# Seven block products in place of eight on the way up through a gated feed-forward layer (Macaron block, one Trainium2 core)

## The chip, the core and the metric

The kernel runs on one core of one Trainium2 chip. The core has a matrix engine (TensorE; PE in the profile, with its weight loads as PEld), a vector engine (VectorE, DVE), a scalar engine (ScalarE, ACT), a general engine (GpSimd, POOL), and a queue that issues most transfers (SyncE, SP). All work on a shared on-chip memory of 128 partitions; PE writes its sums to eight accumulation banks, which DVE and ACT read. The metric is the time in microseconds (us) of one execution; the median of three runs is compared.

## What is computed

`x` is [2, 512, 512]: 1024 rows of 512 features, float32. Six residual parts follow one another. The first and the third are the gated feed-forward layer that the change is in, with the same weights; between them lies a state-space layer, after them come a small memory layer, an attention layer and the memory layer again.

```python
def _L0_ffn_ref(x, w1, s1, w2, s2, w3, s3):
    ...
    W1 = dequant_q40(w1, s1, hidden, dim)      # hidden = 1376, dim = 512
    W3 = dequant_q40(w3, s3, hidden, dim)
    W2 = dequant_q40(w2, s2, dim, hidden)
    a = jnp.einsum('bsd,hd->bsh', x, W1)
    b = jnp.einsum('bsd,hd->bsh', x, W3)
    h = jax.nn.silu(a) * b
    return jnp.einsum('bsh,dh->bsd', h, W2)
...
x = x + 0.5 * _L0_ffn_ref(_layernorm(x, axis=-1), ...)
x = x + _L0_attn_ref(_layernorm(x, axis=-1), ...)
x = x + 0.5 * _L0_ffn_ref(_layernorm(x, axis=-1), ...)
```

The weights come packed: one int32 holds two signed 4-bit values, and one float scale belongs to 64 values. `dequant_q40` takes both nibbles out, multiplies by the scales and lays the values out in order.

## The kernel before

**Rows and tiles.** The 1024 rows are eight tiles `x[t]` of 128 rows by 512 features, four to each of the two batches. A layer first normalises the tiles (`norm_parts`, L130 to L185): on each tile the statistics (L142, L143, DVE), the root (L146, ACT), the reciprocal (L163, DVE), the centring (L153, DVE), then four transposes on PE (L175) and a copy by ACT (L179) into `hT[b]`, which holds a batch with the features on the partitions, as four blocks of 128 features by 512 rows.

**Going up.** The 1376 middle units are padded to 11 tiles of 128. For each tile `ht`, `ffn` takes the two up weights `w1` and `w3` (each four blocks of 128 features by 128 units), and for each batch forms `pa` (`fa` in the trace) and `pb` (`fb`), four f32 products of 128x128 by 128x512 each (L298). ACT takes the tanh of half of `pa` (L303), DVE makes (tanh + 1) * pa (L305) and multiplies by `pb` (L308): the gated value `act`, twice what silu(a) * b is. A tile thus has 16 products in each pass.

**Going down.** For each of the eight row tiles, 11 products add up in a bank (`fo`, L317), and DVE adds a quarter of it to `x[t]` (L321). In the first pass the next layer's normalisation of the tile follows right behind.

**The weights.** In the first pass (`n == 0`) they are unpacked: SP loads the packed values and the scales (`unpack_in`: four transfers of 128 KB for one up weight; `unpack_out`: one of 256 KB and four of 64 KB for a down weight), DVE takes out the nibbles (two operations of 64x512 for an up weight, L222 and L213; sixteen of 32x128 for a down weight), and multiplies by the scales (L241, L261). The unpacked tile is also written to HBM by ACT's queue (`keep`, L281), and the second pass (`n == 1`) loads it from there (`wk`, L120 and L125). The buffers for packed values and for scales have three slots each, up weights share 20 slots with the weights of the state-space layer, down weights 12.

**What sets the order.** Each engine works in order. Most of the program is put in order by a list scheduler that looks for what is ready, and may pull an operation ahead of earlier ones of another stage. Inside `in_order()` the order of PE, DVE, ACT and POOL is that of the program text. Before the change this holds for the down products, but not for the norm, the unpacking and the up products of the feed-forward layers, which the scheduler orders: in the first pass it runs the unpacking of the down weights between the gating operations of the later tiles. SP's order is the scheduler's in both versions. The accumulation banks are named by tags: `mm`, `dd`, `y` and `tr` have two each during the feed-forward layers.

Of the kernel before, what the change touches and what calls it, by code (L numbers as in the profile page):

```python
# [10 lines left out]
F32 = mybir.dt.float32  # L11
# [3 lines left out]
AF = mybir.ActivationFunctionType  # L15
ALU = mybir.AluOpType
AX = mybir.AxisListType

P = 128
NB, S, D = 2, 512, 512  # L20
NT = NB * S // P
NC = S // P
KD = D // P
# [2 lines left out]

HID = 1376
NHT = 11


NH, HP, NG = 128, 64, 8
# [12 lines left out]
class Step:  # L44


    def __init__(self, g, b, q):
        self.g, self.b, self.q = g, b, q
        self.ct = g * PAIRS + q
        self.h0 = 2 * self.ct  # L50
        self.n = f"{self.ct}_{b}"
# [7 lines left out]
class Kernel:  # L59
    def __init__(self, tc, ctx, a, out):  # L60
        self.tc, self.nc, self.a, self.out = tc, tc.nc, a, out
        nc = self.nc
        self.const = ctx.enter_context(tc.tile_pool(name="const", bufs=1))
        self.xpool = ctx.enter_context(tc.tile_pool(name="xpool", bufs=1))
        self.dram = ctx.enter_context(
            tc.tile_pool(name="scratch", bufs=1, space=bass.MemoryType.DRAM)
        )
        masks = self.const.tile([P, 4, P], F32, name="masks")
        nc.sync.dma_start(out=masks, in_=a["masks"])
        self.ident = masks[:, 0, :]  # L70
        self.upper = masks[:, 1, :]
        self.below = masks[:, 2, :]
        self.ones = masks[:, 3, :]
        self.eps = self.const.tile([P, 2], F32, name="eps")
        nc.vector.memset(self.eps[:, 0:1], EPS)
        nc.vector.memset(self.eps[:, 1:2], 4.0 * EPS)
        self.npool = ctx.enter_context(tc.tile_pool(name="npool", bufs=1))
        self.x = []
        for t in range(NT):
            xt = self.xpool.tile([P, D], F32, name=f"x{t}", tag=f"x{t}")  # L80
            nc.sync.dma_start(out=xt, in_=a["x"][t * P : (t + 1) * P, :])
            self.x.append(xt)

    @contextmanager
    def ssm_const(self):
# [158 lines left out]
    def unpack_out(self, pool, ht):  # L244

        nc = self.nc
        wi = pool.tile([P, D], I32, tag="wi", name=f"wi2_{ht}", bufs=3)
        sc = pool.tile([P, D], F32, tag="sc", name=f"sc2_{ht}", bufs=3)
        nc.sync.dma_start(out=wi, in_=self.a["q2"][ht])
        for qd in range(4):  # L250
            rows = slice(qd * 32, qd * 32 + 32)
            nc.sync.dma_start(
                out=sc[rows], in_=self.a["s2"][ht, qd].partition_broadcast(32)
            )
            cols = wi[rows].rearrange("p (a e) -> p e a", e=4)
            for e in range(4):

                low = ((43 * e + qd) // 2) % 2 == 1
                self.nibble(cols[:, e, :], cols[:, e, :], low)
        wt = self.w2pool.tile([P, D], F32, tag="w2", name=f"w2_{ht}")  # L260
        nc.vector.tensor_tensor(out=wt, in0=wi, in1=sc, op=ALU.mult)  # L261
        return wt

    def ffn(self, n, then=None):

        tc, nc = self.tc, self.nc
        first = n == 0
        if first:
            self.kept = {}

        def weight(which, ht):
            if first:
                t = (
                    self.unpack_out(pool, ht)
                    if which == 2
                    else self.unpack_in(pool, which, ht)
                )
                keep = self.dram.tile(
                    list(t.shape), F32, name=f"keep{which}_{ht}", tag=f"k{which}_{ht}"
                )  # L280
                nc.scalar.dma_start(out=keep, in_=t)  # L281
                self.kept[which, ht] = keep
                return t
            load = self.w2 if which == 2 else self.w
            return load(self.kept[which, ht], f"wk{which}_{ht}")

        with tc.tile_pool(name=f"ffn{n}", bufs=2) as pool:
            hT = self.norm(f"f{n}")
            act = []
            for ht in range(NHT):  # L290
                w1, w3 = weight(1, ht), weight(3, ht)
                g = pool.tile([P, NB, S], F32, tag=f"act{ht}", name=f"act{n}_{ht}", bufs=1)
                for b in range(NB):
                    pa = self.ps("mm", [P, S], f"fa{n}_{ht}_{b}")
                    pb = self.ps("dd", [P, S], f"fb{n}_{ht}_{b}")
                    for dst, wt in ((pa, w1), (pb, w3)):
                        for k in range(KD):
                            nc.tensor.matmul(  # L298
                                dst, lhsT=wt[:, k, :], rhs=hT[b][:, k, :],
                                start=k == 0, stop=k == KD - 1,  # L300
                            )
                    th = pool.tile([P, S], F32, tag="th", name=f"th{n}_{ht}_{b}", bufs=3)
                    nc.scalar.activation(th, pa, AF.Tanh, scale=0.5)  # L303

                    nc.vector.scalar_tensor_tensor(  # L305
                        out=th, in0=th, scalar=1.0, in1=pa, op0=ALU.add, op1=ALU.mult
                    )
                    nc.vector.tensor_tensor(out=g[:, b, :], in0=th, in1=pb, op=ALU.mult)  # L308
                act.append(g)
            w2 = [weight(2, ht) for ht in range(NHT)]  # L310
            with self.in_order():
                parts = then() if then is not None else None
                for t in range(NT):
                    b, c = divmod(t, NC)
                    po = self.ps("mm", [P, D], f"fo{n}_{t}")
                    for ht in range(NHT):
                        nc.tensor.matmul(  # L317
                            po, lhsT=act[ht][:, b, c * P : (c + 1) * P], rhs=w2[ht],
                            start=ht == 0, stop=ht == NHT - 1,
                        )  # L320
                    nc.vector.scalar_tensor_tensor(  # L321
                        out=self.x[t], in0=po, scalar=0.25, in1=self.x[t],
                        op0=ALU.mult, op1=ALU.add,
                    )
                    if parts is not None:
                        hT, start, turn = parts
                        start(t)
                        if t > 0:
                            turn(t - 1)
            return parts  # L330

    def in_order(self):
# [1059 lines left out]
def masks():  # L1392
    i = np.arange(P)
    m = np.zeros((P, 4, P), np.float32)
    m[:, 0] = i[:, None] == i[None]
    m[:, 1] = i[:, None] <= i[None]
    m[:, 2] = i[:, None] > i[None]
    m[:, 3] = 1
    return m
# [42 lines left out]
    return w.reshape(o // P, P, i // P, P).transpose(0, 3, 2, 1)  # L1442


def pad_hidden(v, axis):
    to = [(0, 0)] * v.ndim
    to[axis] = (0, NHT * P - HID)
    return np.pad(v, to)


def layout(v):
    a = {"x": v["L0_attn_x"].reshape(NB * S, D), "masks": masks()}
    later = np.arange(P)[:, None] < np.arange(P)[None]
    a["later"] = np.tile(later, (1, NC)).astype(np.float32)
    for n in (1, 3):
        w = pad_hidden(v[f"L0_ffn_w{n}"].reshape(HID, KD, 64), 0)
        s = pad_hidden(v[f"L0_ffn_s{n}"].reshape(HID, KD, 2), 0)
        a[f"q{n}"] = w.reshape(NHT, P, KD, 64).transpose(0, 3, 2, 1)
        a[f"s{n}"] = s.reshape(NHT, P, KD, 2).transpose(0, 3, 2, 1)
    w = v["L0_ffn_w2"]  # L1460
    w = pad_hidden(np.concatenate([w, w], axis=1).reshape(D, HID).T, 0)
    a["q2"] = w.reshape(NHT, P, D)

    s = np.repeat(v["L0_ffn_s2"], 2).reshape(D, HID // 32).T
    s = np.pad(s, ((0, NHT * 4 - HID // 32), (0, 0)))
    a["s2"] = s.reshape(NHT, 4, D)

    a["w_in"] = w_tiles(v["L0_attn_in_proj_w"])
# [9 lines left out]
        axis=1,  # L1478
# [23 lines left out]
    i = np.arange(P)  # L1502
# [24 lines left out]
```

## Time and profile before

| | us |
|---|---|
| median of three runs (lowest, highest) | 2854.03 (2848.28, 2856.74) |
| the profiled execution's own time | 2862.34 |
| its span, first to last instruction | 2860.6 |
| pass 1 of the feed-forward layer: first up product, first down product, end | 17.62, 169.06, about 247 |
| state-space layer | about 247 to 2160 |
| pass 2: first up product, first down product, end | 2169.84, 2323.87, about 2399 |
| memory, attention, memory | about 2399 to 2860 |
| mean granted clock of PE, share of full speed | 0.974 |

The span is what the profiler saw of one execution, and its own time lies 1.7 us above it. Busy shares count instructions from start to end; PE's records are pipelined, so that a record of 592 ns can be followed by the next after 429 ns, and one f32 product is two records. "Idle before" is the time in which an engine did nothing ahead of a group, with what released it. The granted clock is 1.00 at full speed.

### The profile page before, as it was taken

The page shows a single profiled execution, that of the slowest core. Times are in us where ns is not written, and L with a number is a line of the kernel's source. Part 1 is how long each engine was busy: PE and PEld are TensorE (multiplying, and loading weights), DVE is VectorE, ACT ScalarE, POOL GpSimd, SP SyncE. Part 2 cuts the span into 40 slices and gives each one's busy share as a digit, 9 for nine tenths or more (in the row PEclk, how much of TensorE's full clock was granted, in tenths as well). Part 3 has the DMA queues.
Part 4 walks back from the last instruction along what each step waited for, and adds up shares of the span by engine and source line. Part 5 has one row for each costly group of instructions (what it writes and reads, how often), then busy time and mean ns, then how long its engine had stood idle before and what let it go on. Part 6 is the DMA issues. An engine that isn't in the chain of part 4 may idle for free. (4 is left out here: it accounts for less than half of the span.)

```text
span 2860.6 us, 33568 instructions
## 1 busy us (share of the span) xinstructions
PE 2740.4 (96%) x12288; PEld 1420.1 (50%) x12288; DVE 1988.6 (70%) x3635; ACT 1070.8 (37%) x2355; POOL 529.8 (19%) x348
## 2 busy tenths in 40 slices
PE   8998899999999999999999999999998999788987
PEld 4444455555555555555555555555554444444443
DVE  6824777877888788787788788878882224555545
ACT  1012444444444344344444444434542002244332
POOL 0001112323323222131332322312220000100000
PEclk9999999999999999999999999999999999889986
DMA  8602223223223322322322422332230010000000
GB/s 243 208 33 81 87 87 129 96 76 133 94 82 118 114 81 102 127 85 90 128 92 75 139 96 82 111 122 81 90 110 15 0 49 33 0 1 1 1 1 30
DMA packets 75620, 237.78 MB, mean 83 GB/s; under 512 B 9824, under 2 KB 10400, under 8 KB 58944
## 3 DMA queue, kind: packets, MB, share of 16 engines
q1 hardware_dynamic: 70416, 226.00, 22.9%
q10 hardware_dynamic: 4752, 8.65, 0.8%
q8 instruction: 98, 1.61, 0.2%
q0 software_dynamic: 288, 0.98, 0.1%
q14 instruction: 66, 0.54, 0.1%
HBM read 223.80 MB, written 11.80 MB: 82 GB/s over the span
## 5 line engine op out<-in xcount | busy, mean ns | idle before, releaser
L509 PE MATMUL pg<-hT_s,wi 128*128 128x512 f32 x1024 | 472.3, 604 | 14.6 <-issue 6.9
L509 PE MATMUL cp_h<-hT_s,wi 128*128 128x512 f32 x1024 | 462.9, 595 | 0.0
L698 PE MATMUL po<-wo,yg 128*128 128x512 f32 x1024 | 460.7, 593 | 1.6 <-DVE yg L768 1.6
L600 DVE TENSOR_TENSOR_SCAN M<-rows,later 128x512 f32<-128x512 f32 x256 | 457.4, 1825 | 0.0
L775 POOL TENSOR_TENSOR ssum<-ssum,sq 128x512 f32<-128x512 f32 x112 | 142.5, 1272 | 1237.3 <-ACT sq L774 1237.3
L509 PEld LDWEIGHTS pg<-hT_s,wi 128*128 128x128 f32 x1024 | 184.3, 189 | 222.4 <-issue 214.6
L523 DVE SCALAR_TENSOR_TENSOR acc_h<-cp_h,small,acc_h 128x511 f32<-128x511 f32 (+2 forms) x384 | 286.2, 745 | 9.1
L509 PEld LDWEIGHTS cp_h<-hT_s,wi 128*128 128x128 f32 x1024 | 185.5, 191 | 185.1 <-issue 185.1
L698 PEld LDWEIGHTS po<-wo,yg 128*128 128x128 f32 x1024 | 184.8, 190 | 185.5 <-issue 183.6
L616 POOL TENSOR_TENSOR Cs<-CT,rows 128x768 f32<-128x768 f32 x128 | 254.6, 1989 | 46.3 <-DMA rows<-rows 31.5
L685 DVE SCALAR_TENSOR_TENSOR st<-st,dec_whole,st 128x64 f32<-128x64 f32 x512 | 108.8, 274 | 131.2 <-ACT st L680 131.2
L528 ACT ACTIVATE th_h<-acc_h 128x512 f32<-128x512 f32 x128 | 80.6, 630 | 296.4 <-DVE acc_h L523 296.4
L645 ACT ACTIVATE hd<-ht,dec_end 128x64 f32<-128x64 f32 x768 | 171.1, 324 | 38.3 <-DVE hc L637 38.3
L774 ACT ACTIVATE sq<-yg 128x512 f32<-128x512 f32 x112 | 70.7, 631 | 288.6 <-DVE yg L768 288.6
L614 DVE TENSOR_TENSOR M<-M,CB 128x512 f32<-128x512 f32 x256 | 164.5, 684 | 0.1
L605 ACT ACTIVATE M<-M 128x512 f32<-128x512 f32 x128 | 80.8, 631 | 193.2 <-DVE M L600 193.2
L637 DVE TENSOR_TENSOR hc<-ht,dt 128x512 f32<-128x512 f32 x128 | 88.1, 689 | 90.2 <-PE ht L792 90.2
L1265 DVE CUSTOM_DVE_ANT_0 j<-s,future 128x384 f32<-128x384 f32 (+3 forms) x256 | 112.8, 487 | 53.3 <-PE s L1255 53.1
L749 PEld LDWEIGHTS py<-M,hc 128*64 128x64 f32 x2048 | 109.2, 136 | 66.9 <-issue 64.7
L675 PEld LDWEIGHTS st<-hd,Btok 128*128 128x128 f32 x768 | 103.7, 191 | 75.0 <-issue 39.9
L749 PE MATMUL py<-M,hc 128*64 128x128 f32 x2048 | 140.1, 279 | 0.0
L740 POOL TENSOR_TENSOR x<-x,add 128x512 f32<-128x512 f32 x64 | 97.0, 1545 | 142.6 <-ACT add L738 142.6
(283 smaller groups left out, 3753.0 us busy)
## 6 DMA issues: line engine op xcount, KB each, us to landing
rows<-rows SPq DMA_DIRECT2D x128, 1024.0 KB, 4.7
wi<-in_w_in_dram SPq DMA_DIRECT2D x144, 256.0 KB, 2.8
wo<-in_w_out_dram SPq DMA_DIRECT2D x64, 256.0 KB, 3.4
keep<-w ACTq DMA_DIRECT2D x33, 256.0 KB, 3.5
wk<-keep SPq DMA_DIRECT2D x33, 256.0 KB, 2.7
wi<-in_q_dram SPq DMA_DIRECT2D x44, 128.0 KB, 3.9
sc<-in_s_dram SPq DMA_DIRECT2D x44, 128.0 KB, 3.9
wi<-in_q_dram SPq DMA_DIRECT2D x11, 256.0 KB, 2.8
```

The costliest lines, as they stand in the source:

```text
L509: self.nc.tensor.matmul(p, lhsT=wt[:, k, :], rhs=self.hT[b][:, k, :], start=k == 0, stop=k == KD - 1)
L523: self.nc.vector.scalar_tensor_tensor(out=acc[:, s:], in0=p[:, : S - s], scalar=w[:, 3 - s : 4 - s], in1=acc[:, s:], op0=ALU.mult, op1=ALU ...
L600: self.nc.vector.tensor_tensor_scan(out=m, data0=rows[:, i, 0, :], data1=self.later, initial=0.0, op0=ALU.add, op1=ALU.mult,)
L614: self.nc.vector.tensor_tensor(out=m, in0=m, in1=sh["CB"], op=ALU.mult)
L616: self.nc.gpsimd.tensor_tensor(out=cur.Cs, in0=sh["CT"][:, P:].unsqueeze(1).to_broadcast([P, 2, S - P]), in1=cur.rows[:, :, 1, P:], op=ALU ...
L645: nc.scalar.mul(hd[:, c, ch], p1.pt[:, c, ch], self.dec["dt_end"][:, b * NC + c, h0 + i : h0 + i + 1],)
L675: nc.tensor.matmul(pst[:, c, :], lhsT=self.sh[p1.g, p1.b]["Btok"][:, c, :], rhs=hd[:, c, :], start=True, stop=True,)
L685: nc.vector.scalar_tensor_tensor(out=st[:, c, ch], in0=st[:, c - 1, ch], scalar=self.dec["whole"][:, p1.b * NC + c, h : h + 1], in1=pst[:, ...
L698: nc.tensor.matmul(self.po[c], lhsT=p2.yg[:, c * P : (c + 1) * P], rhs=self.wo[p2.ct], start=p2.q == 0, stop=p2.q == PAIRS - 1,)
L749: nc.tensor.matmul(py[ch, cs], lhsT=hc[:, c, ch], rhs=p1.M[i].rearrange("p (c t) -> p c t", c=NC)[:, c, :], start=c == 0, stop=c == 0, ski ...
L775: nc.gpsimd.tensor_tensor(out=self.ssum, in0=self.ssum, in1=sq, op=ALU.add)
L1265: nc.vector.tensor_tensor_reduce(out=junk[:, :nk], in0=ps[y][:, at[i]], in1=self.future[:, S - nk :], scale=1.0, scalar=-3e38, op0=ALU.add ...
```

## The change

**The block product.** For one tile of middle units, take the up weights as a 2x2 block matrix: the two weights by the two halves of the features (blocks 0 and 1, blocks 2 and 3). Take the rows as another: the two halves of the features by the two batches. The four results (a and b, batch 0 and batch 1) are then a 2x2 by 2x2 block product, eight half products of two PE products each. The change writes it with seven (Strassen's method in Winograd's form, which shares sums): 14 PE products. Tile 0 stays as it was. Sums of the rows are formed once in a layer (`T`, four of 128x1024), sums of the weights once per tile and pass (`s` and `u`, two tiles with four sums of 128x256). Some sums of products are formed by letting PE go on adding in one bank `x`, out of which ACT copies the value in between (three times a tile: into `g`, `u2` and `u4`); the others are DVE additions.

**The order.** After the change, the whole layer is in `in_order()`. Batch 0 is normalised, the first up weights are unpacked, tile 0's products of batch 0 run, then batch 1 is normalised and tile 0's products of batch 1 run. After that, each tile has three parts: `begin` (four products from batch 0 alone), `middle` (six), `end` (four), and the `begin` of a tile stands ahead of the `end` of the tile before. The weights of the next tile are taken between, one down weight per tile at its end, and the writes of unpacked weights (`keep`) at fixed places. `x[4]` to `x[7]` are loaded behind the first up weights.

**The middle units** are reordered in blocks of 32 on the host (`hidden_tiles`), the same in w1, w3 and w2, so that all rows of a down weight's tile have the same nibble pattern. Then a tile's nibbles come out in two operations of 128x256 in place of sixteen of 32x128 (in two tiles of the eleven, in four operations). The unpacking of the up weights is unchanged.

```diff
-        self.x = []
-        for t in range(NT):
-            xt = self.xpool.tile([P, D], F32, name=f"x{t}", tag=f"x{t}")
-            nc.sync.dma_start(out=xt, in_=a["x"][t * P : (t + 1) * P, :])
-            self.x.append(xt)
+        self.x = [
+            self.xpool.tile([P, D], F32, name=f"x{t}", tag=f"x{t}") for t in range(NT)
+        ]
+        self.load(0)
+
+    def load(self, b):
+        for t in range(b * NC, (b + 1) * NC):
+            self.nc.sync.dma_start(out=self.x[t], in_=self.a["x"][t * P : (t + 1) * P, :])
...
-            cols = wi[rows].rearrange("p (a e) -> p e a", e=4)
-            for e in range(4):
-
-                low = ((43 * e + qd) // 2) % 2 == 1
-                self.nibble(cols[:, e, :], cols[:, e, :], low)
+        for kind, r0, r1 in HIDDEN[ht][1]:
+            cols = wi[r0:r1].rearrange("p (a e) -> p a e", e=4)
+
+            for low in (False, True):
+                e = [e for e in range(4) if ((43 * e + kind) // 2 % 2 == 1) == low]
+                part = cols[:, :, e[0] : e[1] + 1 : e[1] - e[0]]
+                self.nibble(part, part, low)
...
+        def product(dst, w, x, start=True, stop=True):
+
+            for k in range(2):
+                nc.tensor.matmul(
+                    dst, lhsT=w[:, k, :], rhs=x[:, k, :],
+                    start=start and k == 0, stop=stop and k == 1, skip_group_check=True,
+                )
+
+        def sums(ht):
+
+
+            w1, w3 = weight(1, ht), weight(3, ht)
+            lo, hi = slice(0, 2), slice(2, 4)
+            if ht:
+                s, u = (
+                    self.wpool.tile([P, KD, P], F32, tag="w", name=f"ws{i}{n}_{ht}")
+                    for i in range(2)
+                )
+                tt(s[:, lo], w3[:, lo], w3[:, hi], ALU.add)
+                tt(s[:, hi], s[:, lo], w1[:, lo], ALU.subtract)
+                tt(u[:, hi], w1[:, lo], w3[:, lo], ALU.subtract)
+                tt(u[:, lo], w1[:, hi], s[:, hi], ALU.subtract)
+                ws[ht] = w1, w3, s, u
+            else:
+                ws[ht] = w1, w3
...
+        def gated(g, a):
+
+            th = pool.tile([P, S], F32, tag="th", name="th", bufs=3)
+            nc.scalar.activation(th, a, AF.Tanh, scale=0.5)
+            nc.vector.scalar_tensor_tensor(
+                out=g, in0=th, scalar=1.0, in1=a, op0=ALU.add, op1=ALU.mult
+            )
+
+        def begin(ht):
...
+            product(x, w1[:, :2], hT[0][:, :2], stop=False)
+            nc.scalar.copy(g[:, 0, :], x)
+            product(r2, w1[:, 2:], hT[0][:, 2:])
+            tt(g[:, 0, :], r2, g[:, 0, :], ALU.add)
+
+        def middle(ht):
...
+            product(x, s[:, 2:], T[1], start=False, stop=False)
+            nc.scalar.copy(u2, x)
+            product(r7, u[:, 2:], T[2], stop=False)
+            product(x, s[:, :2], T[0], start=False, stop=False)
+            nc.scalar.copy(u4, x)
+            gated(act[ht][:, 0, :], act[ht][:, 0, :])
+            tt(u4, r7, u4, ALU.add)
+            st[ht] = x, r7, u2, u4
+
+        def end(ht):
...
+            product(x, u[:, :2], hT[1][:, 2:], start=False)
+            product(r7, w3[:, 2:], T[3], start=False)
+            gated(g[:, 1, :], x)
+            tt(g[:, 1, :], g[:, 1, :], u4, ALU.mult)
+            tt(u2, r7, u2, ALU.add)
+            tt(g[:, 0, :], g[:, 0, :], u2, ALU.mult)
+
+        with tc.tile_pool(name=f"ffn{n}", bufs=2) as pool, self.in_order():
...
+            def norms(b, then=()):
+                ts = range(b * NC, (b + 1) * NC)
+                for t in ts:
+                    stats(t)
+                    root(t, t + 1)
+                    if t > ts[0]:
+                        over(t - 1, t)
+                        centre(t - 1)
+                        turn(t - 1)
+                over(ts[-1], ts[-1] + 1)
+                centre(ts[-1])
+                turn(ts[-1])
+
+            norms(0)
+            sums(0)
+            if first:
+                self.load(1)
+            p0 = plain(0, 0)
+            norms(1)
+            p1 = plain(0, 1)
+            for b, (pa, pb) in enumerate((p0, p1)):
+                g = act[0][:, b, :]
+                gated(g, pa)
+                tt(g, g, pb, ALU.mult)
+
+            tt(T[0], hT[1][:, :2], hT[0][:, :2], ALU.subtract)
+            tt(T[1], hT[1][:, 2:], T[0], ALU.subtract)
+            sums(1)
+            tt(T[2], hT[1][:, 2:], hT[1][:, :2], ALU.subtract)
+            tt(T[3], hT[0][:, 2:], T[1], ALU.subtract)
+            keep()
+            w2.append(weight(2, 0))
+            for ht in range(1, NHT):
+                begin(ht)
+                if ht > 1:
+                    end(ht - 1)
+                keep()
+                if ht + 1 < NHT:
+                    sums(ht + 1)
+                middle(ht)
+                w2.append(weight(2, ht))
+            keep()
+            end(NHT - 1)
```

In `stats` and the rest, the steps of the norm are those of the kernel before. `plain` is the old product of tile 0 for one batch. The host's layout of w1, w3, w2 and their scales follows the new order of the middle units.

## The prediction, made before the change was run

> **What bounds the kernel now.** The page's first part says which engine is full, and the table of stages says it stage by stage.
>
> ```profile
> PE 2740.4 (96%) x12288; PEld 1420.1 (50%) x12288; DVE 1988.6 (70%) x3635; ACT 1070.8 (37%) x2355; POOL 529.8 (19%) x348
> ```
>
> Busy times of stages (start:end, length, then PE, PEld, DVE, ACT and POOL with instruction counts, granted clock, DMA share, GB/s); the rows are the up products of the first and of the second feed-forward pass:
>
> ```profile
> 17.60:168.60 151.00, 150.99 (x353) 66.71 (x352) 102.23 (x293) 16.50 (x26) 0.00 (x0) 1.00 0.64 201
> 2173.20:2323.40 150.20, 150.20 (x351) 66.51 (x350) 29.54 (x43) 16.31 (x26) 0.00 (x0) 1.00 0.01 4
> ```
>
> PE never pauses in either, at a granted clock of 1.00. A busy row alone could hide slack, so the timeline of PE gives the rate:
>
> ```profile
> 2179.67 3.60 PE L298 MATMUL fa<-hT_f,wk 128*128 128x512 f32 x8
> 2183.10 3.60 PE L298 MATMUL fb<-hT_f,wk 128*128 128x512 f32 x8
> ```
>
> Eight records start 3.43 us apart: 0.429 us a record, and an f32 product of 128x128 by 128x512 is two records (176 of `fa` for 88 products), 0.858 us. Fewer products mean less time, if PE stays fed. In pass 1 the feeder is DVE, which also unpacks:
>
> ```profile
> L213 DVE TENSOR_SCALAR wi<-wi 32x128 int32<-32x128 int32 x88 | 21.1, 270 | 0.4
> L222 DVE TENSOR_SCALAR wi<-wi 32x128 int32<-32x128 int32 x88 | 20.9, 269 | 0.1
> L241 DVE TENSOR_TENSOR w<-wi,sc 128x512 f32<-128x512 int32 x22 | 15.2, 691 | 2.4 <-DMA sc<-in_s_dram 1.6
> L305 DVE SCALAR_TENSOR_TENSOR th<-th,fa 128x512 f32<-128x512 f32 x22 | 15.1, 686 | 22.1 <-ACT th L303 21.9
> L213 DVE TENSOR_SCALAR wi<-wi 64x512 int32<-64x512 int32 x22 | 9.3, 424 | 8.9 <-DMA wi<-in_q_dram 8.3
> L261 DVE TENSOR_TENSOR w<-wi,sc 128x512 f32<-128x512 int32 x11 | 7.6, 689 | 0.2
> ```
>
> **The products.** A tile of 128 middle units has 16 products before (32 records, 13.73 us), and 14 after (28 records, 12.01 us). Tile 0 stays plain; ten tiles in two passes save 20 x 1.72 = **34.3 us**. All of it is on the path, since PE is the path. What gives some back:
>
> **DVE, per tile of pass 1.** Seven operations of 128x512 at 0.69 (the combining and gating) 4.8 us; two up weights, 2 x (0.42 + 0.41 + 0.69) = 3.0; four weight sums of 128x256; w2: two nibble operations in place of sixteen, and one product 0.69. The trace has no sum of two SBUF operands at 128x256; the nearest row is a 128x256 product:
>
> ```profile
> L1338 DVE TENSOR_TENSOR O<-po,r x16: 424/425/425, 2531.3 to 2779.7; 128x256 f32<-128x256 f32 x16
> ```
>
> So four sums are 1.7 us (1.1 by the 128-wide nibble row's 0.27, 2.8 by the 512-wide row's 0.69). A strided nibble operation on 128x256 lies between 0.27 and 0.69; I take 0.42, the 64x512 row. w2 is then 1.5 us against 16 x 0.27 + 0.69 = 5.0. Together 11.1 us against 12.0 of PE: DVE just fits. In order it goes like this, counted from PE's start on a tile: r2 is done at 3.4, x and r7 of the tile before at 5.1 and 6.9; DVE ends the four operations on these at 8.9, has the next tile's w1 at 10.4, w3 at 12.0 and the sums at 13.7. PE wants w1 at 12.0 and the first sums at 18.9. The cover is 1.6 us; past it each us costs 9 us over nine tiles. In pass 2 nothing is unpacked, DVE has 6.5 us of 12.
>
> After the change ACT has five operations of 0.60 a tile (three copies, two tanh), 3.0 us, and three issues of 0.33; before, it waits on PE for 84.5 us of pass 1 (table of waits). Two of its copies read a bank that PE adds to next; 1.71 us of other products lie between, against 0.60 and two hand-overs of 0.2 (PE's end to the next start is 0.2 in the trace). Only after the last tile is nothing between: 1.0 us in each pass.
>
> **DMA.** Per tile 3 x 512 KB in and 3 x 256 KB out, 2.3 MB in 12 us, 192 GB/s; the stage at 30 to 60 us ran 254 GB/s. The three unpacking buffers come free one tile ahead, 4 us at worst from issue to landing. Nothing. The loads of pass 2 hang on free weight slots, which two sums per tile now share; 20 slots hold at least three tiles. Nothing, up to 1 us a tile if slots come free late.
>
> **The start of pass 1.** Before, the first up product starts at 17.62. After: DVE norms batch 0 alone, 4 x (0.69 + 0.18 + 0.15 + 0.54) = 6.2 us from 4.2 with 1.2 of waiting for the second tile of x, 11.6; w1 1.5; PE at 13.2. Batch 0 of tile 0 takes 6.9, to 20.1. But ACT's order is fixed after the change: the root of tile 6 stands behind the copy of tile 4, whose transposes stand on PE behind all of batch 0's products. From 20.1 the chain is transposes 0.6, copy 0.6, root 0.3, copy 0.6, root 0.3, reciprocal 0.16, centring 0.55, transposes 0.6, copy 0.6, 4.3 and hand-overs: 4.8, to 24.9 (3 to 7 as bounds). Batch 1 of tile 0: to 31.8. Then DVE, behind the gating, forms T0 and T1 (128x1024; 1.22 each by the slope between 0.425 at 256 and 0.69 at 512) before it unpacks tile 1's w1: 0.69 + 2.44 + 1.52 + hand-overs, PE idle to 36.8. That idle time has a second price, the clock:
>
> ```profile
> 2164.00:2168.00 4.00, 1.44 (x7) 1.03 (x5) 3.01 (x10) 1.90 (x6) 2.51 (x3) 0.50 0.00 0
> 2168.00:2174.00 6.00, 5.90 (x19) 4.38 (x20) 1.72 (x6) 2.56 (x5) 0.00 (x0) 0.50 0.01 3
> 2174.00:2178.00 4.00, 4.00 (x11) 1.76 (x10) 0.00 (x0) 1.60 (x3) 0.00 (x0) 0.99 0.00 0
> ...
> 269.00:272.50 3.50, 3.50 (x9) 1.99 (x8) 0.69 (x1) 0.75 (x2) 0.00 (x0) 0.56 0.07 29
> ```
>
> After 3 us of idle PE the granted clock was 0.50, and stayed there 3.5 us in one place and about 10 in the other, 6 of them busy. After 5 us idle I charge half of the shorter, 1.7 (0 to 3, the shorter lost whole or the longer's busy part at half rate). The Trainium skill, "TensorE: Matmul & The Clock Gate", Part 1, has the same gate: half rate after an idle window of about 3.4 us, full rate after a busy one; these rows agree, and by its windows the charge would be half of one window or of two, 1.7 or 3.4, an estimate. It speaks against this change, which puts new pauses into a stage that had none.
>
> Tile 1: 3.43 + 1.7 + 5.14, to 47.1. Nine tiles: 108.1, to 155.2. Last part 1.0 + 3.43, to 159.6. The down products start there and not at 169.06: **9.4 us**.
>
> **The start of pass 2.** The statistics of batch 0 ran at 2065 to 2078 before, in the state-space stage. After, they are in a fixed order, in which the third root follows the first copy. Fixed orders of two stages do pass one another: ACT's exponential of the bias (L469, next stage) ran at 134.10, ahead of the layer's own list. So two tiles may be centred early and two wait for the last copies: PE starts at 2166.8, or at 2169.6 if none is early; I take 2168.0. Then 6.9 + 2.0 at the low clock, 4.8 of pause as above, 6.9, 3.43, 1.0 of waiting for T1, the sums and T2 (no unpacking here), 5.14, 108.1, 4.43: 2310.7, against 2323.87 before: **13.2 us**.
>
> **Sum.** 9.4 + 13.2 = 22.6 us. The down products, the state-space stage and what follows move up unchanged. The profiled execution (2862.34, span 2860.6) becomes 2839.7; it lies 8.3 above the median of 2854.03, which becomes **2831.4**.
>
> **Rivals.**
> - DVE becomes the bound in pass 1. For it: 11.1 of 12.0, and in the stage from 80 to 110 us DVE was busy 29.35 of 30. Against: independent operations of 0.69 start 0.60 apart there. DVE waits inside a tile, from r2's sum at 4.3 to the gating at 6.2 and about 0.5 for the other tanh; if these 2.3 us aren't absorbed, a tile takes 13.4: 9 x 1.4 = 12.6 back, 2844. Chance 0.13.
> - Slower: PE waits in every tile of both passes for ACT's copies out of the bank that it adds to (place: the third product of a tile and the closing one). It costs 18 us for every us of wait; from 1.25 a tile nothing is gained, from 1.74 it is slower by over 0.3%; at 2.0 us it is 36, 2867. For it: PE, ACT and PE again in one bank, twice a tile. Against: 0.7 us of cover and ACT a quarter full. Chance 0.07.
> - The pauses at the starts don't come or are short (x lands earlier with half the loads ahead, no clock loss): 34.3 and 4 of the early start less 5: 33, 2821. Chance 0.10.
>
> The forecast keeps 0.70. Its own spread: pauses 3 to 7 each, clock 0 to 3 each, start 2166.8 to 2169.6, a DVE late by up to half a us a tile: gains of 13 to 30. The range 2822 to 2846 adds the first rival. A change below 0.3% (8.6 us) can't be told from none. Faster 0.84 (forecast, third rival, a third of the first), same 0.09, slower 0.07.
>
> **What the profile will show.** 14 products a tile, 12.0 us apart in pass 2; in pass 1 the same, with DVE over 85% busy and PE's idle time ahead of a tile's first product near nothing. Two pauses of about 5 us at the start of pass 1, one at that of pass 2. Down products from about 160 and 2301 (2310.7 less 9.4). I am wrong if tiles in pass 1 come over 12.5 us apart, if PE's waits on ACT copies show up in the table of waits, or if the clock stays at 0.50 well into the tiles.

## The result and the profile after

The changed kernel takes **2843.12 us** (median of 8 runs, 2835.55 to 2852.85) against 2856.79 us for the kernel before beside it (8 runs, 2848.28 to 2869.43): ratio 0.9946, 95% interval 0.9924 to 0.9968. It is faster by 13.7 us, with the prediction's sign and in its range, and 11.7 us above its point. The profiled execution took 2843.27 us, with a span of 2841.5.

The first part of the page shows fewer PE records (12208 for 12288) and 30.9 us less of busy PE:

```profile
PE 2709.5 (95%) x12208; PEld 1403.3 (49%) x12208; DVE 2037.5 (72%) x3633; ACT 1104.1 (39%) x2415; POOL 529.9 (19%) x348
```

Busy times of stages (columns as in the prediction: start:end, length, PE, PEld, DVE, ACT, POOL, granted clock, DMA share, GB/s): the pause ahead of tile 1, its first products, nine tiles of pass 1 and nine of pass 2.

```profile
34.80:39.60 4.80, 0.13 (x1) 0.00 (x0) 4.53 (x7) 0.00 (x0) 0.00 (x0) 0.91 0.00 0
39.60:43.20 3.60, 3.58 (x5) 1.52 (x6) 3.47 (x8) 0.00 (x0) 0.00 (x0) 0.50 0.66 195
43.20:46.10 2.90, 2.90 (x6) 1.21 (x5) 2.83 (x5) 0.59 (x1) 0.00 (x0) 0.59 0.92 288
51.20:159.40 108.20, 108.20 (x253) 47.69 (x251) 87.62 (x176) 25.96 (x45) 0.00 (x0) 1.00 0.65 210
...
2193.70:2301.90 108.20, 108.20 (x253) 47.69 (x251) 53.34 (x95) 25.96 (x45) 0.00 (x0) 1.00 0.08 22
```

Nine tiles take 108.2 us in either pass, 12.02 each, and PE is busy all that time: the tiles run as reckoned. What went otherwise stands ahead of them. The timeline of PE at the start of pass 1 (start, length, what, and in brackets the idle time before it with what ended it):

```profile
14.59 5.50 PE L354 MATMUL fa<-hT_f,w 128*128 128x512 f32 x8 [0.67 <-ACT hT_f L201]
19.93 3.60 PE L354 MATMUL fb<-hT_f,w 128*128 128x512 f32 x8
23.36 1.04 PE L197 MATMUL hps_f<-masks,h_f 128*128 128x128 f32 x8
25.77 1.35 PE L197 MATMUL hps_f<-masks,h_f 128*128 128x128 f32 x8 [1.38 <-DVE rstd_f L189]
27.80 3.70 PE L354 MATMUL fa<-hT_f,w 128*128 128x512 f32 x8 [0.68 <-ACT hT_f L201]
31.34 3.60 PE L354 MATMUL fb<-hT_f,w 128*128 128x512 f32 x8
39.62 3.78 PE L326 MATMUL fmm<-hT_f,w 128*128 128x512 f32 x4 [4.68 <-DVE w L263]
43.19 3.06 PE L326 MATMUL fdd<-hT_f,w 128*128 128x512 f32 x4
46.09 1.88 PE L326 MATMUL fmm<-T,ws 128*128 128x512 f32 x4
...
160.22 1.98 PE L326 MATMUL fmm<-hT_f,ws 128*128 128x512 f32 x4 [0.68 <-ACT u L389]
```

Both pauses are there (23.36 to 27.80 and 34.77 to 39.62). Two stretches are slow: eight records that take 3.43 us at full speed take 5.34 at the very start (14.59 to 19.93) and 6.47 behind the second pause (39.62 to 46.09). Behind the first pause they take 3.54. These times, like those of eight records below, go from the first start to the start of what follows, which is 0.16 less than the length in a row with nothing idle behind it, as the last record outlasts its slot (0.592 for 0.429). The first down product comes at 163.90, 5.2 us earlier than before. Pass 2 starts so:

```profile
2154.89 1.09 PE L197 MATMUL hps_f<-masks,h_f 128*128 128x128 f32 x8 [0.35 <-ACT r L858]
2159.98 1.09 PE L197 MATMUL hps_f<-masks,h_f 128*128 128x128 f32 x4 [4.00 <-DVE rstd_f L189]
...
2163.15 6.41 PE L354 MATMUL fa<-hT_f,wk 128*128 128x512 f32 x8 [0.68 <-ACT hT_f L201]
2169.40 3.60 PE L354 MATMUL fb<-hT_f,wk 128*128 128x512 f32 x8
```

Two tiles are transposed early and two late, as forecast, and the first eight records take 6.25. The first down product of pass 2 comes at 2306.41, 17.5 us earlier than before.

### The profile page after: what moved, and what is told of

The parts are those of the page before. It is cut to its first block, busy times and chain, and to the rows that moved or that the text cites. A ratio compares the mean times of both kernels' runs of the same rounds, so it can differ in the third digit from the quotient of the medians.

```text
span 2841.5 us, 33439 instructions
## 1 busy us (share of the span) xinstructions
PE 2709.5 (95%) x12208; PEld 1403.3 (49%) x12208; DVE 2037.5 (72%) x3633; ACT 1104.1 (39%) x2415; POOL 529.9 (19%) x348
## 4 chain that ended last, share of the span: by engine, by line
PE 82%; DVE 11%; ACT 4%; issue 2%; POOL 0%; DMA 0%; SPq 0%; ACTq 0%; DVEq 0%; POOLq 0%
PE pg L655 14%; PE po L844 13%; PE cp_h L655 13%; PE fo L463 5%; PE fmm L326 5%; PE py L895 3%; PE st L821 3%; DVE acc_h L669 3%; PE fy L326 2%; PE py L904 2%; PE cp_CT L655 2%; PE cp_BT L655 2%; PE ht L938 2%; PE w L1447 2%; PE av L1463 1%
```

## The experiments

**Theory**: the products bring 34.3 us; the new fixed order at the starts takes back a part, by pauses of PE and by the slow products behind them. **Rivals**: DVE or ACT's copies bind the tiles; or the order is free, and the gain is lost elsewhere. F1 and F2 below are the starts of the first down product in pass 1 and pass 2. Intervals are of the ratio to the kernel before on the same chip. F1 and F2 come from one execution of each kernel. The changed kernel's two executions differ by 0.5 and 1.6 us, and in the seven changed kernels without spare products PE's first up product starts anywhere from 13.45 to 15.17, so that a difference of about a us at F1 says little.

| kernel | F1 | F2 | median, us | ratio, 95% | mean clock, this / before beside it |
|---|---|---|---|---|---|
| before | 169.06 | 2323.87 | 2856.79 | | |
| changed | 163.90 | 2306.41 | 2843.12 | 0.9946 (0.9924 to 0.9968) | |
| changed again | 163.38 | 2307.97 | 2844.68 | 0.9953 (0.9931 to 0.9974) | 0.9742 / 0.9767 |
| all tiles plain | 173.57 | 2331.13 | 2878.62 | 1.0057 (1.0030 to 1.0085) | 0.9726 / 0.9767 |
| sixteen nibble operations | 171.77 | 2314.13 | 2850.48 | 0.9992 (0.9978 to 1.0005) | 0.9747 / 0.9783 |
| copies four times | 174.87 | 2328.72 | 2873.23 | 1.0062 (1.0042 to 1.0081) | 0.9720 / 0.9783 |
| sums ahead | 158.81 | 2301.96 | 2836.81 | 0.9925 (0.9902 to 0.9948) | 0.9752 / 0.9767 |
| spare products | 158.77 | 2298.10 | 2834.26 | 0.9914 (0.9886 to 0.9942) | 0.9785 / 0.9767 |
| roots together | 160.07 | 2299.04 | 2833.44 | 0.9926 (0.9899 to 0.9954) | 0.9763 / 0.9783 |
| tile 1 begun early | 155.20 | 2295.26 | 2833.93 | 0.9929 (0.9915 to 0.9942) | 0.9753 / 0.9783 |
| all together | 154.26 | 2290.03 | 2830.69 | 0.9899 (0.9870 to 0.9927) | 0.9750 / 0.9753 |

### The change once more, and its order alone

> The changed kernel as it is, once more, as the yardstick of this chip. Theory (seven products save 34.3 us, pauses at the starts give about 15 back): ratio to the kernel before 0.993 to 0.996, span near 2841.5, first down products near 163.9 and 2306.4. Rival (the 19 us of the first profile were luck of one execution): ratio 0.998 or more.

It came as expected: F1 163.38, F2 2307.97, 2844.68 us, ratio 0.9953.

```diff
-                begin(ht)
-                if ht > 1:
-                    end(ht - 1)
+                p = [plain(ht, b) for b in range(NB)]
...
-                middle(ht)
+                for b in range(NB):
+                    gate(b, *p[b], ht)
```

> The changed kernel with the plain 16 products in all eleven tiles: the order written out and the reordered middle units without the block product (no T, no weight sums). Theory (the products bring 34.3 us, the order alone costs): pass 1's first down product at 174.5 to 176.5 (34.8, 2.4 of pause, ten tiles of 13.73), 10 to 13 us after the changed kernel's and 5 to 7 after the kernel before's; pass 2 15 us after the changed kernel's; span 2867, ratio to the kernel before 1.002 to 1.005. Rival (the gain comes from the order, the earlier start and the shorter unpacking): span about 2841 as with the block product.

F1 173.57, a us below what was expected, F2 2331.13. Without the seven products the new order costs 4.5 us in pass 1 and 7.3 up to F2, and the kernel is slower than before. The order is not free. The median, 22 us above the kernel before, holds more than that: the mean clock is lower too, 0.9726 against 0.9767. Between this kernel's profiled execution and the changed kernel's first lie 9.7 us at F1 and 24.7 at F2, and not 34.3: here tile 1 waits less, since no sums of rows stand ahead of its weight (2.29 against 4.68):

```profile
36.13 3.70 PE L354 MATMUL fa<-hT_f,w 128*128 128x512 f32 x8 [2.29 <-DVE w L263]
39.67 3.60 PE L354 MATMUL fb<-hT_f,w 128*128 128x512 f32 x8
```

The eight records behind that wait take 3.54, not 6.47. So 2.4 us of wait, 2.9 of slow products, 0.8 at the closing wait and a start of PE that is 1.1 earlier here (13.45) stand against the 17.2 us of pass 1, and leave 10.0, for the 9.7 measured. In pass 2 the waits of 0.9 in tile 1 and 0.8 at the close leave 15.5, for 15.0.

### Is DVE's cover real? w2 by sixteen operations again

```diff
-            for low in (False, True):
...
-                self.nibble(part, part, low)
+            for r in range(r0, r1, 32):
+                cols = wi[r : r + 32].rearrange("p (a e) -> p e a", e=4)
+                for e in range(4):
+                    self.nibble(cols[:, e, :], cols[:, e, :], low)
```

> The changed kernel with w2 unpacked by sixteen operations on 32x128 again in place of two on 128x256. In the trace of the changed kernel two such operations take 0.2 of a us each beyond overlap and DVE is busy 9.74 us of each 12.02; sixteen at 0.21 from start to start are 3.4 us. Theory (DVE has 2.3 us left in a tile, so the mended unpacking is just what keeps it off the path): DVE 12.4 to 13.2 us a tile, PE paused by 0.4 to 1.2 in each tile of pass 1, its first down product 3 to 10 us later than the changed kernel's 163.4 to 163.9; pass 2, which unpacks nothing, keeps its 12.02 us a tile. Rival (the prediction's durations, 11.1 us a tile plus 2.8): 13.9 a tile, 17 us later. Second rival (DVE overlaps more than its busy time shows): nothing, within 1 us.

The theory holds: F1 comes 7.9 us after the changed kernel's. Busy times from 60 to 150 us of this kernel, and PE's wait that recurs from 76.89 on in each tile of pass 1:

```profile
60.00:150.00 90.00, 85.31 (x196) 36.34 (x195) 87.60 (x237) 20.17 (x35) 0.00 (x0) 1.00 0.56 184
```

```profile
89.95 1.98 PE L325 MATMUL fmm<-hT_f,w 128*128 128x512 f32 x4 [0.77 <-DVE w L263]
...
102.98 1.98 PE L325 MATMUL fmm<-hT_f,w 128*128 128x512 f32 x4 [0.75 <-DVE w L263]
```

DVE is busy 97%, tiles come 13.03 us apart, PE waits for the up weight. Pass 2 keeps its rate, and the median is 5.8 and 7.4 us above those of the changed kernel's two sets of runs. The reordering of the middle units is thus what keeps DVE, at 81% in the changed kernel, from becoming the bound in pass 1.

### What would ACT's copies have to cost?

```diff
-            nc.scalar.copy(g[:, 0, :], x)
+            for _ in range(4):
+                nc.scalar.copy(g[:, 0, :], x)
...
-            nc.scalar.copy(u2, x)
+            for _ in range(4):
+                nc.scalar.copy(u2, x)
```

> The changed kernel with each of ACT's two copies out of the bank that PE adds to next done four times (same result, 1.5 us more of ACT per copy), in all tiles but the plain one. It prices the slower rival of the prediction, which did not appear: in the trace of the changed kernel the copy ends 0.93 us ahead of PE's next product into its bank, so with a hand-over of 0.2 about 0.7 us is free; four copies at 0.49 from start to start end 0.54 us after it. Theory: PE pauses 0.5 to 0.8 us at two places in a tile, tiles come 13.0 to 13.6 us apart in both passes, and the kernel takes 20 to 32 us more than the changed kernel, 2863 to 2877, slower than the kernel before. Rival (banks are not held by a read, or the copies run beside it): tiles stay at 12.02 us.

Tiles come 13.10 us apart in both passes, and the kernel is slower than before, as expected, by 0.6%. Not all of that is the copies: F2 lies 4.9 us behind the kernel before, 0.2%, and the four runs have a mean clock of 0.9720 against 0.9783. ACT's copy and then PE, in pass 2 of this kernel:

```profile
2241.33 2.44 ACT L388 COPY u<-fmm 128x512 f32<-128x512 f32 x4 [2.84 <-PE fmm L326]
```

```profile
2243.82 1.98 PE L326 MATMUL fmm<-T,ws 128*128 128x512 f32 x4 [0.81 <-ACT u L388]
```

PE goes on 0.05 us after the fourth copy. A single copy would end at 2241.94 (a quarter of 2.44 after 2241.33), and PE, without the wait, would want the bank 0.97 earlier than 2243.82 (0.81 of idle and the 0.16 by which a record outlasts its slot), at 2242.85: 0.9 us is the cover. Only one place waits, not two: behind the copy into `g`, the `end` of the tile before adds its four products to the two, 5.15 us (6 x 0.858) in all.

### The order on DVE: sums ahead

```diff
-            for b, (pa, pb) in enumerate((p0, p1)):
...
-            tt(T[0], hT[1][:, :2], hT[0][:, :2], ALU.subtract)
-            tt(T[1], hT[1][:, 2:], T[0], ALU.subtract)
-            sums(1)
-            tt(T[2], hT[1][:, 2:], hT[1][:, :2], ALU.subtract)
+            gate(0, *p0)
+            tt(T[0], hT[1][:, :2], hT[0][:, :2], ALU.subtract)
+            tt(T[1], hT[1][:, 2:], T[0], ALU.subtract)
+            sums(1)
+            tt(T[2], hT[1][:, 2:], hT[1][:, :2], ALU.subtract)
+            gate(1, *p1)
```

`gate` is the gating of tile 0 for one batch.

> Only DVE's order at the start of a pass is changed: T0, T1, tile 1's unpacking and its weight sums stand ahead of the gating of tile 0's second batch. Theory (PE's pause before tile 1 and the low clock behind it are one cause): the 4.85 us of pause goes and the 3.0 us of slow products behind it too, first down product of pass 1 at 156, 0.9 us less in pass 2, span 2833, ratio to the changed kernel 0.997. Rival (the products behind the pause are slow for another reason): 4.85 + 0.9 only, first down product at 159, span 2836. Second rival (DVE is the bound at the start): the pause moves to the third product of tile 1, nothing gained.

The pause ahead of tile 1 is gone, but F1 is 158.81, 4.6 and 5.1 us ahead of the changed kernel's two executions, not 7.9: the number of the rival. What is missing is in its timeline:

```profile
28.16 5.40 PE L354 MATMUL fa<-hT_f,w 128*128 128x512 f32 x8 [0.68 <-ACT hT_f L201]
33.39 3.60 PE L354 MATMUL fb<-hT_f,w 128*128 128x512 f32 x8
36.83 1.88 PE L326 MATMUL fmm<-hT_f,w 128*128 128x512 f32 x4
38.54 1.88 PE L326 MATMUL fdd<-hT_f,w 128*128 128x512 f32 x4
...
44.33 1.98 PE L326 MATMUL fmm<-T,ws 128*128 128x512 f32 x4 [0.47 <-ACT u L386]
```

Tile 1's slow products did go with their pause: its first eight records take 3.43 us (36.83 to 40.26). But the eight records behind the other pause, between the batches, take 5.23 here, and took 3.54 in the changed kernel. That pause stands ahead of all that the edit moved on DVE, so the edit is not what slowed them; such a loss comes in some executions and not in others (the next section counts them). And ACT's copy waits behind the write of w2's tile, which waits for its unpacking. F1 alone would thus have spoken for the wrong explanation. In pass 2 the wait in tile 1, 0.9 us, is gone as expected.

### The clock: spare products in the pauses

```diff
+            def warm(times):
+                pw = self.ps("y", [P, S], f"warm{n}_{times}")
+                for _ in range(times):
+                    nc.tensor.matmul(pw, lhsT=self.ident, rhs=self.wide, start=True, stop=True)
```

Three of these stand ahead of pass 1's transposes, five ahead of tile 1, four in pass 2's pause; the order is otherwise the changed kernel's.

> The changed kernel with spare products of the mask tile, whose results nobody reads, in three pauses of PE: 3 ahead of the first transposes of pass 1, 5 in the pause before tile 1 of pass 1, 4 between the second and third tile's transposes of pass 2. The pauses stay. Theory (slow products are the price of idle PE): tile 0's first eight records in pass 1 take 3.4 us for 5.3, tile 1's first four products 3.4 for 6.5, tile 0's first eight in pass 2 3.4 for 6.3: 7.8 us less, span 2834. Rival (they are slow because of transfers or hand-overs): nothing gained, up to 1 us lost where spare products run over.

```profile
3.21 4.24 PE L434 MATMUL warm<-masks 128*128 128x512 f32 x6 [3.21 <-DMA masks<-in_masks_dram]
...
12.01 3.67 PE L355 MATMUL fa<-hT_f,w 128*128 128x512 f32 x8 [0.88 <-DVE w L264]
...
23.40 5.24 PE L355 MATMUL fa<-hT_f,w 128*128 128x512 f32 x8 [0.68 <-ACT hT_f L202]
...
36.76 1.98 PE L327 MATMUL fmm<-hT_f,w 128*128 128x512 f32 x4 [0.40 <-DVE w L264]
...
2157.54 3.70 PE L355 MATMUL fa<-hT_f,wk 128*128 128x512 f32 x8 [0.68 <-ACT hT_f L202]
```

PE does more work and the kernel is faster, by 4.6 and 5.1 us at F1 and by 9.9 and 8.3 at F2, against the two executions of the changed kernel. Where the pause was filled, eight records take 3.51 and 3.54 us in pass 1 and 3.54 in pass 2; behind the one pause of pass 1 that was left empty they take 5.08. That settles it: the slow products are the price of PE standing idle, not of the data.

How often that price falls due can be counted over the ten profiled executions of the changed kernel and its variants (three of them are below). A pass's first eight records are slow in all fifteen places where nothing fills the idle time ahead of them (4.94 to 6.59 us), and in none of the five where spare products do (3.50 to 3.54). Behind the four pauses of 4.85 ahead of tile 1 they are slow each time (5.2 to 6.5), behind the fourteen pauses of 4.4 between the batches four times (5.08 to 5.24, else 3.54), behind the four that are cut to 3.1 never.

### ACT's order: roots together

```diff
+            def together(b):
+                t0, t1 = b * NC, (b + 1) * NC
+                for t in range(t0, t1):
+                    stats(t)
+                root(t0, t1)
+                over(t0, t1)
...
-            norms(1)
+            together(1)
```

> The version with the sums ahead (DVE unpacks tile 1 before T2 and T3), and in addition the statistics, square roots and reciprocals of a batch stand together ahead of the copies out of its transposes: batch 1 in both passes, batch 0 also in the second pass. Theory (the pauses of 4 to 5 us at the starts come from the fixed order on ACT and DVE: the root of a row tile stands behind the copy of another): the pause between batch 0 and batch 1 falls from 4.4 us to 2.3 to 3.0 in each pass (transposes and copies are left in it), and the 4.0 us pause ahead of the second pass's first product goes. Pass 1's first down product at 156 to 158 (158.81 without this edit), pass 2's at 2293 to 2297 (2301.96), span 2822 to 2830. Rival (the pauses come from DVE, which does the four tiles' statistics and centring in one run anyway): pause still 4 us or more, both times within 1 us of the version without this edit. Since the clock loss moves between the pauses by up to 3 us, the pauses themselves decide, not the total alone.

The pauses went the theory's way, though not all of it: 24.21 to 27.31 (3.1 us, with transposes and copies in it) in place of 4.4, just above the 2.3 to 3.0 expected, and pass 2's wait of 4.00 is 2.05, halved and not gone. F1 did not follow: 160.07, since ACT's copy in tile 1 now waited 2.19 us behind the write of w2's tile, with slow products behind that:

```profile
43.89 3.68 PE L326 MATMUL fmm<-T,ws 128*128 128x512 f32 x4 [2.19 <-ACT u L386]
```

F2 came at 2299.04, 2.9 us before the version with the sums ahead alone, and 2 us later than expected.

### Tile 1 begun early

```diff
-            product(x, u[:, :2], hT[1][:, 2:], start=False)
+            if ht < NHT - 1:
+                product(x, u[:, :2], hT[1][:, 2:], start=False)
             product(r7, w3[:, 2:], T[3], start=False)
+            if ht == NHT - 1:
+                product(x, u[:, :2], hT[1][:, 2:], start=False)
...
+            begin(1)
+            p1 = plain(0, 1)
```

> All that the runs so far point to in one kernel: sums ahead, roots together, tile 1's first two products (batch 0 alone, hT of batch 0) between batch 0 and batch 1 of tile 0, three spare products of the mask at the start of the first pass, and in the last tile the product that needs no copy ahead of the one that waits. Theory (the start and its clock are the only losses left; tiles run at the rate of PE): pass 1's first down product at 150 to 154, pass 2's at 2284 to 2292, span 2814 to 2824, ratio to the kernel before 0.985 to 0.990. Rival (the loss of clock comes back in other pauses of the stages behind, whatever is mended at the starts): the first down products move as said, but the time stays at 2830 or above.

F1 155.20 and F2 2295.26, 1.2 and 3.3 us beyond what was expected. Batch 1 of tile 0 no longer waits, but the next product does, 3.00 us, because ACT's exponential of the bias, which belongs to the next layer and was pulled ahead, waited for its transfer (8.14 us idle). The median of 2833.93 and the profiled span of 2837.1 (2814 to 2824 expected) agree with the rival, though the first down products moved less than either expected. Pass 2's start has no spare products here, and its first eight records take 6.38 us.

### All together

This has the sums ahead, the roots together, spare products in the two pauses ahead of the first products, and in tile 1 the writes behind the copies:

```diff
-                keep()
+                if ht > 1:
+                    keep()
                 if ht + 1 < NHT:
                     sums(ht + 1)
                 middle(ht)
+                if ht == 1:
+                    keep()
```

> The version with sums ahead and roots together, with two additions: three spare products of the mask ahead of the first pass's transposes and four in the second pass's pause between transposes (into a bank that nothing reads), and in tile 1 the stores of unpacked weights issued behind ACT's two copies instead of ahead of them, so that the copy does not wait for w2's unpacking. Within every kernel so far time follows the mean granted clock (about 2.2 us for each 0.001), so two numbers are expected. Theory (what the first down products gained is real, and the rest of the time goes by the clock): pass 1's first down product at 152 to 156 (160.07 without the additions), pass 2's at 2286 to 2292 (2299.04), no wait over 0.5 us in tile 1; at a mean clock of 0.975 the time lies at 2826 to 2832 (2835.7 without), and the median at 2815 to 2830 as the clock falls. Rival (the stages behind lose in clock what the starts gain, so that the median stays at 2833 whatever the starts do): both first down products as said, median 2831 to 2838 and mean clock 0.972 or less.

F1 154.26 and F2 2290.03, both as said; tile 1 has no wait, but tile 2 has one of 1.57 us (for its weight on DVE). At a clock of 0.975 its runs lie at 2830.7 us, as said; the median of 2830.69 lies just above the theory's end and just below the rival's, and decides nothing by itself. Its ratio is the lowest of all, 0.9899. Part of that is no merit of the change: spare products would be open to the kernel before too, which was not tried.

### Where the rest of the time varies

Runs of one kernel differ by up to 30 us, and go by the mean granted clock. Over the 52 runs of the kernel before that stood beside the experiments, time and clock have a correlation of -0.99, and 0.001 of clock is 2.2 us; over 20 of the changed kernel, -0.97 and 2.1. At 0.975 the fitted times are 2862.6 and 2842.7, 19.9 us apart at equal clock. The mean times are 14.3 apart (2858.2 and 2843.9), because the changed kernel's mean clock is lower, 0.9745 against 0.9770, and 0.0025 at 2.15 us per 0.001 is 5.4. So the 19.9 us are not all the change's to claim: a part of the lower clock is its own doing. In the rows of the pause and tile 1 above, 3.4 us of full clock are missing (4.80 x 0.09, 3.60 x 0.50, 2.90 x 0.41), which is 0.0012 of that execution's mean, where the kernel before has a clock of 1.00 up to F1; by 2.15 us per 0.001 this is 2.6 us.

The rest of the spread lies behind F2. Up to F2 the eleven profiled executions have a clock of 0.98 to 1.00, behind it one of 0.87 to 0.91, and the stretch behind F2 takes from 545.9 us (all tiles plain, 0.87) down to 529.5 (sums ahead, 0.91). These are stages that the change doesn't touch. The 35 us that begin 75 us after F2, in the first memory layer, where PE runs the same instructions in the same order; first of before, then of after:

```profile
2398.90:2433.90 35.00, 33.30 (x132) 15.60 (x130) 26.36 (x87) 17.79 (x35) 5.23 (x12) 1.00 0.19 66
```

```profile
2381.40:2416.40 35.00, 33.32 (x110) 15.28 (x108) 24.25 (x74) 15.82 (x31) 5.22 (x12) 0.85 0.18 66
```

1.00 against 0.85, 132 records against 110. From F2 to the attention layer's first product it took 131.1 us before and 136.0 after, but 130.9 with the sums ahead and 140.0 with the spare products: no sign of the change. Why the mean clock is lower there is not settled. It may be the change's new pauses: the seven kernels of the table that leave one of the two starts unfilled lie 0.0015 to 0.0063 below the kernel before beside them, the two that fill the starts of both passes at +0.0018 and -0.0003. But nothing was run that sets the clock of the later stages by itself.

## Why the prediction was right, and where it was off

**The products: right.** 12.02 us a tile in both passes, 12.01 predicted.

**DVE: the conclusion was right, its size was off.** The groups of the changed kernel from 51.2 to 159.4 us (count, busy, mean ns, idle before):

```profile
L285 DVE TENSOR_TENSOR w<-wi,sc 128x512 f32<-128x512 int32 x9 | 6.2, 691 | 0.3
...
L321 DVE TENSOR_TENSOR ws<-w,w 128x256 f32<-128x256 f32 x9 | 3.8, 418 | 0.0
...
L235 DVE TENSOR_SCALAR wi<-wi 128x256 int32<-128x256 int32 x7 | 2.0, 288 | 0.0
```

The sum of the weights takes 0.42, as the product of 128x256 did. The strided nibble operation takes 0.29, near the lower bound of 0.27, not the 0.42 that was taken. By single durations a tile is 10.8 us, against 11.1; by busy time it is 9.74 (87.62 / 9), because independent operations overlap. DVE is busy 81% of that stretch, where over 85% was forecast. The rival of DVE as the bound would have needed 2.3 us more, and the run with sixteen operations shows it.

**ACT's copies: right in the tiles.** The cover is 0.9 us at one place and 5.15 at the other, where the forecast puts 1.71 of products at both. Only the last tile waits, 0.8 us in each pass for 1.0 predicted. But the price of the rival was named by a gain that didn't come in full: with 1.08 us a tile more the kernel is already slower, where the forecast puts that point at 1.74; 0.2% of the 0.6 stand at F2, and the rest goes with that run's lower clock.

**The start of pass 1: 5.2 us gained, 9.4 predicted. This term failed.** PE starts at 14.59 and not at 13.2 (+1.4): DVE waits 1.8 us for x's second tile, not 1.2, and another 0.6 for the last root, which stands behind a copy on ACT; and the last copy, which PE waits for, follows transposes that take 1.1 us a tile, for 0.63 in the run with spare products. Batch 0 of tile 0 takes 8.77 for 6.9 (+1.9). The pauses take 4.4 and 4.85 for 4.8 and 5.0 (-0.5). The clock behind the second takes 3.0 for 1.7 (+1.3). The rest is within 0.2; together 4.3. All pauses were foreseen. The pauses' clock came at the upper end of the 0 to 3 that were given. What the working had no term for is that PE is slow at the kernel's first products, where no earlier work stands. The clock column is no guide at the first place: it shows 1.00 from 14.60 to 19.93, where eight records took 5.33. The Trainium skill, "TensorE: Matmul & The Clock Gate", Part 1, has a half-rate clock as the state at rest and a window that runs free of the kernel, so that the loss depends on where in it a product lands. The runs agree that it varies: at the same first eight records the loss was 1.7 to 3.2 us in the seven kernels without spare products ahead of them (1.9 in the changed kernel, 3.2 in the same kernel run again), and 0.1 in the three with them. Where in a window the products fell, no run shows.

**The start of pass 2: 12.3 us, 13.2 predicted.** Products start 0.7 later than the 2168.0 taken (counted from the state-space layer's end), the clock costs 2.8 for 2.0, the pause 4.4 for 4.8, the wait in tile 1 0.9 for 1.0; the state-space layer before it came 0.4 earlier.

**The sum and its conversion.** In the profiled executions the gain is 19.1 us (2862.34 to 2843.27) for 22.6: 5.1 short at F2, and 1.6 back behind it, where the later stages took 535.1 us in place of 536.7. The median misses by 11.7, and the larger part of that is the last step, in which 8.3 were taken off for the median. The profiled execution of before had a mean clock of 0.974, low among the 52 runs beside the experiments (median 0.977). The changed kernel's is typical, 0.15 us above its median. So 8.2 us of the miss (8.31 less 0.15) came from treating the distance between one execution and the median as a constant, where it was that execution's clock.

**The range: in part luck.** 2843.12 lies inside 2822 to 2846 only because the range was drawn wider for the first rival, which did not come. The forecast's own spread, gains of 13 to 30, ends at 2841 from the 2854.03 it started from; the gain of 13.7 over the runs beside it is at its lower edge.

**The rivals.** DVE as the bound and the waits on copies did not appear; the pauses did come, against the third.

## What to carry to other kernels

Price a pause of PE twice, as its length and as up to 3 us of half-speed products behind it, and price the first products of a kernel at the low speed. Behind pauses of one length that second price came in some executions and not in others, so read what an edit did at the place that it changed, and not from a later total alone. Look at what else stands in the queue ahead of the copy or root that PE waits for. Before a profiled execution's time is set against a median, compare its mean granted clock with those of the other runs.

## What was not expected of the hardware

- The mean granted clock goes with nearly all of the spread between runs of one kernel (correlation -0.99): 0.968 to 0.982, 2877 to 2847 us for the kernel before.
- Twelve spare products, two records each, made the kernel faster by 10 us in the median (2844.68 to 2834.26) and by 8.3 to 9.9 at the first down product of pass 2.
- A strided int32 nibble operation on 128x256 takes 0.29 us, hardly more than one on 32x128 (0.27).
- Of fourteen like pauses of 4.4 us between PE's products (transposes fill a part of them), four had slow products behind them and ten had none.
